# Fourier stage, last part: spectra of equal moving factor added on VectorE before the inverse transform along x

## The chip, the cores and the metric

The kernel runs on one core of one Trainium2 chip. The metric is the device time of one execution in microseconds. The engines have short names here, as in the profile: PE is TensorE's matmuls and PEld its weight loads, DVE is VectorE, ACT is ScalarE, POOL is GpSimd, SP is SyncE.

## The reference

The program is four layers of a metaformer on an input of 4 x 64 x 64 x 128 numbers in 32 bits. Every layer has a mixing part and a feed-forward part. The change lies in the mixing part of layer 2, a Fourier neural operator. Its last part works on 4 x 32 images of 128 x 128 points and applies, twice, one layer of this kind (`m0` and `m1`):

```python
def _spectral_conv(x, w2, oh, ow):
    w = w2[..., 0] + 1j * w2[..., 1]
    X = jnp.fft.rfft2(x, norm='forward')
    Xk = jnp.concatenate([X[:, :, :mh, :mw], X[:, :, -mh:, :mw]], axis=2)
    Yk = jnp.einsum('bixy,ioxy->boxy', Xk, w)
    ...
    return jnp.fft.irfft2(out, s=(oh, ow), norm='forward')

m = _fno_layer(an, m0cw, m0sw, H, W, inner_norm=True, act=True)
m = _fno_layer(m, m1cw, m1sw, H, W, inner_norm=True, act=False)
out = _inorm(m, mon_w, mon_b) + a
```

For each image, then: a transform to a few modes, a complex weight for each mode, a transform back, a normalization over the image, a scaled copy of the input added, and, in the first of the two layers, a Gelu.

## The kernel before

The stages of the four layers follow each other on one core. `stage_fourier` holds the Fourier operator, and its last part is a loop over 16 groups of images: four batches with four groups each, `group(b, g, pT)`, and eight tiles of 128 x 128 numbers in a group. All numbers are 32-bit floats.

A group is a Python generator. Its steps are cut by `yield`, and a loop at the end of the stage starts a new group every seven rounds and moves every active group on by one step each round. So the instructions of two or three groups alternate in the order in which they are recorded. A scheduler then settles the order on each engine; on an engine, instructions run in that order. Semaphores join the engines.

One group does this, with the lines of the profile:

- It loads its skip images (`sk`), adds the input image to them on POOL (L2089), and computes an inverse transform from `pT` (L2094, `ra`, `dya`) that is added (L2101). `pT` is rebuilt for each batch by 64 transposes (L2143, L2144).
- `image_stats` takes the moments (L2039 to L2053, with one matmul `pm`, L2044), `inv_std` and `shift` make scale and bias from them (L2058 to L2066), and `apply` writes eight tiles on ACT (L2071).
- `add_to_x` adds a result to the running x on POOL, in two instructions (L2079).
- For each of two layers it calls `spectral(m, mw[layer])`, then takes statistics of the result, applies the scale, adds the scaled input (L2125) and, in the first layer, applies the Gelu on ACT (L2127).

`spectral` is where the change is made. It handles a group in two halves of four tiles. For each half:

- four matmuls `prf` (L2006) transform along y; ACT copies the result to SBUF (`fr`, L2008);
- a matmul `pz` (L2014) transforms along x into a PSUM tile of 66 rows;
- DVE multiplies it by the weights in four instructions (L2018). The result is `m`, a tile named `w` in the profile, of 66 partitions with the axes u, c and 512 elements: `u` names which of two moving factors `rx[:, u, :]` the product meets in the inverse, and `c` the real or the imaginary part of the spectrum;
- `terms` makes the inverse along x: for each pair of images `j`, four matmuls (L2028) accumulate in one PSUM tile `pi`, over `u` and `c`;
- ACT copies `pi` (`ir`, L1991), and a matmul `pf` with `dyq` (L1997) ends the inverse along y.

The four products of one half are written so:

```python
nc.vector.tensor_tensor(
    m[:, u, c], window(pz, 32 * c, [[64, 8], [0, 2], [1, 32]]),
    window(f, 128 * u + 64 * c, [[0, 8], [32, 2], [1, 32]]), op=ALU.mult,
)
```

A matmul of 32-bit numbers leaves two records in the profile, so a call of `spectral` has 64 records at L2028, and the 32 calls have 2048.

Of the kernel before, what the change touches and what calls it, by code (L numbers as in the profile page):

```python
# [13 lines left out]
ALU = mybir.AluOpType  # L14
# [346 lines left out]
def window(ap, off, dims):  # L361

    return bass.AP(ap.tensor, ap.offset + off, [list(ap.ap[0])] + dims)
# [1191 lines left out]
def stage_fourier(k, a):  # L1555
# [11 lines left out]
    nc, tc = k.nc, k.tc  # L1567
    with ExitStack() as octx:
# [3 lines left out]
        def load(pool, name, shape, src=None, eng=None):  # L1572
            t = pool.tile(shape, F32, tag=name, name=name)
            (eng or nc.sync).dma_start(t, a[name] if src is None else src)
            return t
# [6 lines left out]
        rx = load(wp, "rx", [66, 2, 128])  # L1582
# [30 lines left out]
        with ExitStack() as ctx:  # L1613
# [8 lines left out]
            with ExitStack() as ctx2:  # L1622
# [76 lines left out]
                for b in range(4):  # L1699
# [50 lines left out]
                    for q in range(8):  # L1750
                        px = ps.tile([128, 4, 2, 33], F32, tag="pt", name="pxt")
                        for j in range(4):
                            for c in range(2):
                                for e in range(2):
                                    mark = nc.tensor.matmul(
                                        px[64 * e : 64 * e + 64, j].rearrange("p c m -> p (c m)"), rt[:, :, c, 32 * e + 4 * q + j], fw[:, c, :],
                                        start=(c == 0), stop=(c == 1),
# [29 lines left out]
            with ExitStack() as ctx2:  # L1787
                yp = ctx2.enter_context(tc.tile_pool(name="fo_y", bufs=3))
                ps = ctx2.enter_context(tc.tile_pool(name="fo_pss", bufs=2, space=PSUM))
                for hg in range(4):  # L1790
                    hs = slice(8 * hg, 8 * hg + 8)
                    acc = [ps.tile([128, 8, 64], F32, tag=f"acc{bp}", name=f"acc{bp}") for bp in range(2)]
                    for g in range(17):
                        n = 128 if g < 16 else 64
# [19 lines left out]
                    for bp in range(2):  # L1814
                        o = att[:, bp, hs, :]
                        m = yp.tile([128, 8, 1], F32, tag="m", name="m")
# [10 lines left out]
        with ExitStack() as ctx:  # L1827
# [58 lines left out]
            with ExitStack() as ctx2:  # L1886
# [25 lines left out]
                for q in range(16):  # L1912
                    acc = [ps.tile([128, 3, 132], F32, tag="acc", name=f"acc{bp}") for bp in range(2)]
                    for hp in range(16):
                        n = 2 * q + hp // 8
# [20 lines left out]
                    if q >= 8:  # L1936
                        u = sm.tile([128, 2, 4, 66], F32, tag="u", name="u")
# [15 lines left out]
        with ExitStack() as ctx:  # L1953
# [4 lines left out]
            for i in range(2):  # L1958
# [3 lines left out]
                for u in range(2):  # L1962
                    p, n = mc[:, 2 * u], mc[:, 2 * u + 1]
# [19 lines left out]
            def inverse(terms, dyi):  # L1983

                rs = []
                for h in range(2):
                    pi = ps.tile([128, 4, 128], F32, tag="pr", name="pi")
                    for j in range(4):
                        terms(pi[:, j, :], h, j)
                    r = sm.tile([128, 512], F32, tag="ir", name="ir", bufs=6)  # L1990
                    nc.scalar.copy(r, pi.rearrange("p j x -> p (j x)"))  # L1991
                    rs.append(r)
                yield
                pfs = []
                for r in rs:
                    pf = ps.tile([128, 4, 128], F32, tag="pf", name="pf", bufs=4)
                    nc.tensor.matmul(pf, dyi, r, start=True, stop=True)  # L1997
                    pfs.append(pf)
                return pfs

            def spectral(src, f):
                rs = []
                for h in range(2):
                    pr = ps.tile([128, 4, 128], F32, tag="pr", name="prf")
                    for j in range(4):
                        nc.tensor.matmul(pr[:, j, :], src[:, 4 * h + j, :], dyp, start=True, stop=True)  # L2006
                    r = sm.tile([128, 512], F32, tag="ir", name="fr", bufs=6)
                    nc.scalar.copy(r, pr.rearrange("p j c -> p (j c)"))  # L2008
                    rs.append(r)
                yield  # L2010
                ms = []
                for r in rs:
                    pz = ps.tile([66, 8, 2, 32], F32, tag="pr", name="pz")
                    nc.tensor.matmul(pz, fwp, r, start=True, stop=True)  # L2014
                    m = sm.tile([66, 2, 2, 8, 2, 32], F32, tag="w", name="w")
                    for u in range(2):
                        for c in range(2):
                            nc.vector.tensor_tensor(  # L2018
                                m[:, u, c], window(pz, 32 * c, [[64, 8], [0, 2], [1, 32]]),
                                window(f, 128 * u + 64 * c, [[0, 8], [32, 2], [1, 32]]), op=ALU.mult,  # L2020
                            )
                    ms.append(m)
                yield

                def terms(out, h, j):
                    for u in range(2):
                        for c in range(2):
                            nc.tensor.matmul(  # L2028
                                out, ms[h][:, u, c, 2 * j : 2 * j + 2].rearrange("p n a y -> p (n a y)"), rx[:, u, :],
                                start=(u == 0 and c == 0), stop=(u == 1 and c == 1),  # L2030
                            )

                return (yield from inverse(terms, dyq))

            def image_stats(src):
# [45 lines left out]
            def group(b, g, pT):  # L2081
# [36 lines left out]
                for layer in range(2):  # L2118
                    yield
                    pfs = yield from spectral(m, mw[layer])  # L2120
                    mean, var = yield from image_stats(halves(pfs))
                    r = inv_std(var)
                    y = tile8("m", 6)
                    apply(y, halves(pfs), r, shift(mean, r, 0.0))
                    nc.vector.scalar_tensor_tensor(y, m, par[f"m{layer}sw"], y, op0=ALU.mult, op1=ALU.add)  # L2125
                    if layer == 0:
                        nc.scalar.activation(y, y, AF.Gelu)  # L2127
                    m = y
# [20 lines left out]
            while True:  # L2149
                if rounds % 7 == 0 and waiting is not None:  # L2150
                    n = next(waiting, None)
# [738 lines left out]
```

## Time and profile before

| what | value |
|---|---|
| median of three runs | 6653.65 us (6647.25 to 6657.48) |
| the profiled execution, its time | 6648.12 us |
| its span, first to last instruction | 6646.1 us |
| mean granted clock of TensorE | 0.891 |
| PE busy | 5567.9 us, 84% |
| DVE busy | 4479.9 us, 67% |
| ACT busy | 3008.3 us, 45% |
| POOL busy | 2042.6 us, 31% |
| last part of the Fourier stage | 3355 to 4170 us |

The profile is of one execution, so sums are made against its 6648.12 us. Busy time is the time in which an engine has an instruction under way. The groups in part 5 give the line, the engine, the operation and the tiles, then count, total and mean duration, then how long the engine sat idle before them and what ended that. In a timeline each row has start, duration, engine, line, operation, tiles and count, and in brackets the idle time before it and what ended it. "PEclk" is the share of TensorE's full clock that was granted.

### The profile page before, as it was taken

The page shows a single profiled execution, that of the slowest core. Times are in us where ns is not written, and L with a number is a line of the kernel's source. Part 1 is how long each engine was busy: PE and PEld are TensorE (multiplying, and loading weights), DVE is VectorE, ACT ScalarE, POOL GpSimd, SP SyncE. Part 2 cuts the span into 40 slices and gives each one's busy share as a digit, 9 for nine tenths or more (in the row PEclk, how much of TensorE's full clock was granted, in tenths as well). Part 3 has the DMA queues.
Part 4 walks back from the last instruction along what each step waited for, and adds up shares of the span by engine and source line. Part 5 has one row for each costly group of instructions (what it writes and reads, how often), then busy time and mean ns, then how long its engine had stood idle before and what let it go on. Part 6 is the DMA issues. An engine that isn't in the chain of part 4 may idle for free. (4 is left out here: it accounts for less than half of the span.)

```text
span 6646.1 us, 144915 instructions
## 1 busy us (share of the span) xinstructions
PE 5567.9 (84%) x58031; PEld 3066.5 (46%) x58031; DVE 4479.9 (67%) x9659; ACT 3008.3 (45%) x6819; POOL 2042.6 (31%) x1806
## 2 busy tenths in 40 slices
PE   7777888866688858989978876898998998998989
PEld 3336666654456545334456655335235243252233
DVE  6748777754477562859945555884774866847877
ACT  5445555533155312731056565765234343352375
POOL 0002222210010100018921110353553654645645
PEclk9888889887799979989977788997997997989999
DMA  6556888870400022059700000001111111111101
GB/s 160 149 141 209 244 240 243 244 234 29 168 1 1 2 70 57 1 152 185 157 20 11 13 10 1 6 1 46 46 42 50 39 46 46 37 43 50 32 23 32
DMA packets 713463, 545.23 MB, mean 82 GB/s; under 512 B 299360, under 2 KB 624488, under 8 KB 709448
## 3 DMA queue, kind: packets, MB, share of 16 engines
q1 hardware_dynamic: 651464, 482.23, 27.1%
q10 hardware_dynamic: 61312, 53.57, 2.7%
q8 instruction: 463, 7.59, 0.5%
q14 instruction: 224, 1.84, 0.1%
HBM read 366.25 MB, written 152.86 MB: 78 GB/s over the span
## 5 line engine op out<-in xcount | busy, mean ns | idle before, releaser
L2706 DVE TENSOR_TENSOR t<-S,q 128x1536 f32<-128x1536 f32 x512 | 893.8, 1755 | 172.5 <-PE S L2706 172.2
L2706 POOL TENSOR_TENSOR t<-t,q 128x512 f32<-128x512 f32 x512 | 651.6, 1273 | 488.8 <-ACT t L2706 488.8
L2706 ACT COPY t<-S 128x512 f32<-128x512 f32 x512 | 299.7, 585 | 826.3 <-PE S L2706 768.2
L2706 PE MATMUL S<-R,L 32*128 32x512 f32 x4096 | 611.4, 651 | 44.0 <-DMA R<-wd 38.9
L2706 PE MATMUL acc<-t,sum 128*32 128x512 f32 x4096 | 548.0, 608 | 0.6 <-DVE t L2706 0.5
L2422 PE MATMUL pe<-ew,yT 128*128 128x512 f32 x1024 | 487.0, 611 | 27.3 <-DVE xs L2428 24.8
L909 DVE COPY_PREDICATED band<-bit,band 128x384 f32<-128x384 int32 (+11 forms) x384 | 312.4, 923 | 174.7 <-ACT band L900 156.1
L890 PE MATMUL S<-kpad,qm 32*64 32x192 f32 (+3 forms) x8192 | 360.8, 400 | 62.0 <-ACT band L900 23.0
L2428 DVE SCALAR_TENSOR_TENSOR xs<-pe,gate,xs 128x128 f32<-128x128 f32 x1024 | 331.3, 344 | 92.5 <-PE pe L2422 77.6
L2706 PEld LDWEIGHTS S<-R,L 32*128 32x128 f32 x4096 | 178.6, 186 | 462.0 <-ACT t L2706 391.4
L1928 PE MATMUL acc<-w,attT 128*64 128x396 f32 x2048 | 349.0, 500 | 25.7 <-issue 15.0
L2431 ACT ACTIVATE sc<-pe,gate 128x128 f32<-128x128 f32 x1024 | 290.3, 377 | 158.1 <-PE pe L2422 135.3
L1924 DVE TENSOR_TENSOR w<-xp,e 128x1188 f32<-128x1188 f32 x256 | 336.2, 1388 | 33.9 <-ACT xp L1907 14.6
L890 PEld LDWEIGHTS S<-kpad,qm 32*64 32x64 f32 x8192 | 261.4, 150 | 121.1 <-issue 60.4
L1001 PE MATMUL pt<-ident,D 128*128 128x128 f32 x1536 | 259.5, 318 | 64.2 <-DMA D<-dd 51.8
L2422 PEld LDWEIGHTS pe<-ew,yT 128*128 128x128 f32 x1024 | 181.6, 193 | 265.5 <-issue 168.4
L1923 POOL TENSOR_TENSOR w<-xtl,e 128x396 f32<-128x396 f32 x256 | 260.5, 1035 | 119.4 <-DMA e<-ed 75.6
L2028 PE MATMUL pi<-rx,w 66*128 66x128 f32 x2048 | 276.0, 291 | 10.1 <-DVE w L2018 2.9
L2028 PEld LDWEIGHTS pi<-rx,w 66*128 66x128 f32 x2048 | 253.1, 201 | 52.2 <-DVE w L2018 51.3
L1003 ACT COPY dt<-pt 128x512 f32<-128x512 f32 x384 | 205.5, 595 | 145.4 <-PE pt L1001 144.8
L2706 PEld LDWEIGHTS acc<-t,sum 128*32 128x32 f32 x4096 | 81.4, 108 | 391.7 <-issue 366.3
L1928 PEld LDWEIGHTS acc<-w,attT 128*64 128x64 f32 x2048 | 159.7, 137 | 215.1 <-issue 146.5
(529 smaller groups left out, 11442.7 us busy)
## 6 DMA issues: line engine op xcount, KB each, us to landing
vb<-vd SPq DMA_DIRECT2D x272, 256.0 KB
e<-ed SPq DMA_DIRECT2D x64, 792.0 KB
D<-dd SPq DMA_DIRECT2D x128, 192.0 KB
D<-dd SPq DMA_DIRECT2D x128, 168.0 KB
D<-dd SPq DMA_DIRECT2D x128, 144.0 KB
w<-in_e_weight_dram ACTq DMA_DIRECT2D x16, 1024.0 KB
w<-in_e_weight_dram SPq DMA_DIRECT2D x16, 1024.0 KB
D<-dd SPq DMA_DIRECT2D x128, 120.0 KB
```

The lines of the kernel that those rows point to most:

```text
L890: ins = nc.tensor.matmul(acc[g][64 * h : 64 * h + 64].rearrange("p (a s) c -> p a s c", a=3), qm[rows, h, m, :], keys, start=(m == 0), sto ...
L909: nc.vector.copy_predicated(flat[:, :, 0:n], bit[:, 0, :, i : i + 1].to_broadcast([128, 48, n]), flat[:, :, s : s + n])
L1001: ins = nc.tensor.transpose(pt[:, g, :], D[:, g, ty : ty + 382 : 3], k.ident)
L1003: nc.scalar.copy(dt, pt)
L1923: nc.gpsimd.tensor_tensor(w[:, 3:4], planes[q][:, 3:4], wide(1, [[132, 3], [1, 132]]), op=ALU.mult)
L1924: nc.vector.tensor_tensor(w[:, 0:3].rearrange("p b c m -> p b (c m)"), xp[:, q % 2], wide(3, [[1, 396]]), op=ALU.mult)
L1928: nc.tensor.matmul(acc[b // 2][64 * (b % 2) : 64 * (b % 2) + 64].rearrange("p c m -> p (c m)"), attT[:, b // 2, hp, 64 * (b % 2) : 64 * (b ...
L2028: nc.tensor.matmul(out, ms[h][:, u, c, 2 * j : 2 * j + 2].rearrange("p n a y -> p (n a y)"), rx[:, u, :], start=(u == 0 and c == 0), stop= ...
L2422: nc.tensor.matmul(pe[h].rearrange("p e c -> p (e c)"), yT[:, 128 * t : 128 * t + 128], ew[:, 4 * h : 4 * h + 4, :].rearrange("p e c -> p ...
L2428: nc.vector.scalar_tensor_tensor(xt, pe[0][:, e, :], gate[:, t, e : e + 1], xt, op0=ALU.mult, op1=ALU.add)
L2431: nc.scalar.activation(sc[:, e, j, :], pe[1][:, e, :], AF.Copy, scale=gate[:, t, 4 + e : 5 + e])
L2706: last[engine] = f(*args, **kw)
```

## The change

After the four products of a half, one VectorE instruction adds the two products that share the same moving factor (`c` = 0 and 1) for both `u`: 66 partitions, 2 x 512 elements. The sum lies where the product of `c` = 0 lay. `terms` then accumulates over `u` alone: two matmuls for each pair of images in place of four. The rest of the code is the same. The add is L2022 in the changed kernel; the matmul of `terms` is L2028 in both, and no other line that is named here changes its number.

```diff
                                 m[:, u, c], window(pz, 32 * c, [[64, 8], [0, 2], [1, 32]]),
                                 window(f, 128 * u + 64 * c, [[0, 8], [32, 2], [1, 32]]), op=ALU.mult,
                             )
+                    nc.vector.tensor_tensor(m[:, :, 0], m[:, :, 0], m[:, :, 1], op=ALU.add)
                     ms.append(m)
                 yield
 
                 def terms(out, h, j):
                     for u in range(2):
-                        for c in range(2):
-                            nc.tensor.matmul(
-                                out, ms[h][:, u, c, 2 * j : 2 * j + 2].rearrange("p n a y -> p (n a y)"), rx[:, u, :],
-                                start=(u == 0 and c == 0), stop=(u == 1 and c == 1),
-                            )
+                        nc.tensor.matmul(
+                            out, ms[h][:, u, 0, 2 * j : 2 * j + 2].rearrange("p n a y -> p (n a y)"), rx[:, u, :],
+                            start=(u == 0), stop=(u == 1),
+                        )
```

On the built program's order: SP and POOL issue the same instructions in the same order, and no engine's order changes outside this part of the stage.

## The prediction

> **What bounds the kernel now.** I read the page first (parts 1, 2, 5), then the windows view by stage, the timeline of single periods of the stage that is changed, and the clock in steps of 3.41 us. The edited loop runs only from 3355 to 4170 us of the 6646.1 us span; the chain of waits shown for the whole program ends in a later stage, so the edited stage has to be read by itself. It is no bandwidth stage: in it PE is busy 618.1 of 815 us, DVE 433.1, ACT 474.6, and nothing is full.
>
> The page has the edited matmuls, and the groups by shape have the row nearest to the new add:
>
> ```profile
> L2028 PE MATMUL pi<-rx,w 66*128 66x128 f32 x2048 | 276.0, 291 | 10.1 <-DVE w L2018 2.9
> ...
> L2664 DVE TENSOR_TENSOR s<-s,rs 128x1024 f32<-128x1024 f32 x32 | 37.4, 1209 | 36.8 <-PE pz L2659 36.6 <-issue 0.2
> ```
>
> There are two records for each matmul of the code: 64 records a call of `spectral`, 32 calls. The stage repeats itself: one Gelu (L2127) per group of images, sixteen in all, and between two of them lie two calls, first that of layer 1 of the older group (A), then that of layer 0 of the younger (B). I call this a period. Of the first fourteen, Gelu to Gelu, nine take 45.3 to 46.4 us; two take 57; three hold the transposes that build the next pT and take 53.0, 53.1 and 61.8. The fifteenth takes 44.2, and 35 us follow the last Gelu. The windows of one short and one long period:
>
> ```profile
> core 0: us, PE busy (x) PEld busy (x) DVE busy (x) ACT busy (x) POOL busy (x), PEclk, DMA share, GB/s
> 3799.16:3844.46 45.30, 34.26 (x220) 25.85 (x220) 26.43 (x96) 28.63 (x66) 7.57 (x6) 0.88 0.04 12
> 3642.84:3699.94 57.10, 46.13 (x220) 34.55 (x220) 26.76 (x96) 28.82 (x67) 7.62 (x6) 0.65 0.03 10
> ```
>
> The reader is to see the same instructions on all engines, 11.8 us apart, and a granted clock of 0.88 against 0.65: what PE's clock does in this stage is worth more than its instruction count. The timeline of the short period (Gelu starts at 3798.08) gives the path:
>
> ```profile
> 3799.19 3.58 PE L2006 MATMUL prf<-dyp,m 128*128 128x128 f32 x16 [6.89 <-ACT m L2127]
> ...
> 3803.66 4.87 DVE L2018 TENSOR_TENSOR w<-pz,f 66x512 f32<-66x512 f32 x8 [1.95 <-PE pz L2014]
> ...
> 3804.48 8.46 PE L2028 MATMUL pi<-rx,w 66*128 66x128 f32 x64
> ...
> 3812.78 1.95 PE L2006 MATMUL prf<-dyp,m 128*128 128x128 f32 x16
> ...
> 3814.56 1.88 PE L1997 MATMUL pf<-ir,dyq 128*128 128x512 f32 x4
> ```
>
> PE starts on the first products 0.8 us after VectorE, streams through all 64 records, and goes straight on to prf, pf, pz and call B. The first prf of the period runs at half clock (3.58 us against 1.95 later). In the long period it is call B that runs so:
>
> ```profile
> 3664.20 12.38 PE L2028 MATMUL pi<-rx,w 66*128 66x128 f32 x60
> ...
> 3681.26 3.25 PE L2094 MATMUL pi<-ra,pT 66*64 66x128 f32 x26
> ```
>
> against 7.34 and 1.74 us in the short one. Spacing of pi records from the weight loads: 6.55/58 = 0.113 us at full clock, 11.49/58 = 0.198 at half. The granted clock changes only on a grid of 3.41 us; so in steps of it:
>
> ```profile
> core 0: us, PE busy (x), PEclk, DMA share, GB/s
> 3662.46:3665.88 3.42, 3.08 (x19) 1.00 0.03 7
> 3665.88:3669.29 3.41, 3.41 (x18) 0.50 0.00 0
> ...
> 3819.48:3822.89 3.41, 3.30 (x27) 1.00 0.00 0
> 3822.89:3826.30 3.41, 3.41 (x33) 1.00 0.02 5
> ```
>
> The step before the drop held 15 records of pi, two of pm and two of pz that end in it (0.44 us); the step of 27 records, nearly all pi, kept the clock. And once it is halved, pi at 18 records a step (PE full) did not bring it back in the steps to 3686; 128-row matmuls (prf, pf) filling a step do, as at each period's start. So some 16 pi records in a step are too few.
>
> **The change, part by part.** The order of the built program stays the same on SP and POOL and outside this stage; PE, DVE and ACT differ in it alone.
>
> *Removed*: 32 of 64 records a call, 3.6 us of PE at 0.113. *Added*: two adds a call on VectorE over 66x1024 elements, both operands in SBUF; by L2664 1.2 us each (0.69 by L2101's 512 elements, 1.28 by L2125's 1024 with a scalar; L2664 has the same operation and size), 64 of them, 77 us. VectorE has room for these in 815 us; what counts is where they stand. The scheduler puts the first after five products, the second after the other three. *Moved*: each half's pi waits for all of its products and its add, and PE, in order, holds prf (A) or pi from pT (B) behind it. In B, pm now goes ahead of pi (free: pi waits longer), and pf of the first half goes between the two halves of pi, so it waits for an ACT copy.
>
> *Call A*, from the Gelu's start: products start at 5.58, spacing 0.60; five end at 8.7, add to 9.9, three to 11.7, add to 12.95. pi of half 0: 9.95 to 11.75; of half 1: 13.0 to 14.8. Before, prf began at 14.70. So at full clock the call gains nothing: +0.1 us. But PE now idles from the end of pz (6.56) to 9.95 and again from 11.75 to 13.0; every step of 3.41 us that covers most of the first gap has at most about 1.7 us of pz or 16 pi records. By the step at 3662 the clock drops by 12.4 at the latest. Then half 1 takes 16 x 0.198 = 3.2: +1.5 in all. prf at half clock (3.58 for 1.95): +1.6. prf and pf together then fill a step and bring the clock back within pf: +0.9 (0 to 1.7).
>
> *POOL*: its two adds xs<-xs,sk start at 8.99 and 10.53, beside the new adds. Such a collision exists in the trace: v<-mv is 0.17 us free and
>
> ```profile
> 3837.67 1.26 POOL L2079 TENSOR_TENSOR xs<-xs,m 128x512 f32<-128x512 f32 x1 [21.55 <-ACT m L2071]
> ...
> 3838.12 0.83 DVE L2051 TENSOR_TENSOR v<-mv 128x8 f32<-128x8 f32 x1
> ```
>
> beside POOL's add, ending with it; the products, with one operand in PSUM, are 0.67 with and without. The wait costs 0 to 1.2 a period; I take 1.0, since POOL, pushed back by the first add, ends its second near 12.7, where the second new add wants 11.7. So call B's products start 1.5 + 1.6 + 0.9 + 1.0 = 5.0 later: 24.2 for 19.26.
>
> *Call B*, from its first product: two statistics stand among the products, five end at 3.3, add to 4.5, three to 6.3, one reduction, add to 7.75. The clock has dropped again (one to two steps nearly empty). pi half 0 to 7.7, copy 0.7, pf 1.8 to 10.2, pi half 1 3.2 to 13.4, pi from pT 1.11 + 3.25 to 17.8, pf and two pf of the other inverse 2.0 + 3.6 to 23.4, pm to 24.0; from the last pm to the next Gelu the long period took 9.9 (3688.94 to 3698.86). 24.2 + 24.0 + 9.9 = 58.1: +12.8 on 45.3.
>
> *Sum*: nine short periods x 12.8 = 115; the two of 57, now some 58.4, 3; with pT, 62.9 for 53.0 twice and 61.8 once, 21; the two last periods and the start, with fewer or other calls behind them, 14 (0 to 25). 153 us on a profiled time of 6648.1 gives 6801; that execution is 5.5 us under the median 6653.65, inside the three runs' own spread of 10, so I say 6800 and carry no more.
>
> *A rule against the trace.* The step at 3662, in which PE had work in most of it, halved the clock. The Trainium skill, TensorE: Matmul & The Clock Gate, Part 1, says that the slow state comes after at least one idle window of about 3.4 us. By that rule the 3.4 us gap in A would hardly fill one, the clock would mostly stay, and the time would be that of rival 1; I go by the trace's step.
>
> **Rivals.**
> 1. *The clock stays full.* Then A costs 0.1 + 1.0 (POOL), and in B the variance and with it layer 1's apply (ACT, L2071) come 2.0 later, as both adds stand ahead of it on VectorE: +3.1 x 15 = 46, and the three long periods fall to the short ones (-11, -11, -9): +15, about 6665. For it: the drop hit only three calls before. Against: those calls had more pi records in a step than any call will have now. 0.08.
> 2. *A drops, B recovers*, in half or more of the periods: +5 to +8 each, 75 to 100 in sum: 6725 to 6750. The clock's steps run free of the kernel, so this differs by period. 0.17.
> 3. *Faster: the adds are cheap and the clock holds.* At L2101's 0.69 us for 512 elements instead of 1.2, A ends 1.05 earlier (13.65), B's delay is 1.0, no collision stays, and the long periods go: -31, about 6620. It decides if the add is under 0.8 us. Against: the same operation at 1024 elements is 1.21. 0.05.
>
> **How the numbers follow.** Forecast 6800 with 0.70: range of its own 6760 to 6850 (pf 0 to 1.7, POOL 0 to 1.2, the ends 0 to 25, and the clock coming back a step later). Down through rival 2 to part of rival 1, 6690 to 6850 leaves out about 0.18 (rivals 1 and 3, and the far tail). A measurement of this kernel can tell about 0.2% (13 us) from no change. Rival 1's 6665 lies at the edge of it: 0.05 same, 0.03 slower; rival 3 makes faster 0.05; slower 0.90.
>
> **What would show it.** In the profile after: L2022 x64 near 1.2 us; L2028 at 1024 records; periods of 57 to 60 us all alike; granted clock of the stage near 0.65 instead of 0.81; prf of call B at 3.5 us instead of 1.95; stage end some 150 us later, other stages unchanged. Periods of 48 us at 0.88 would make rival 1 right; an add well under 1 us would make rival 3's price right; periods above 62 would mean that pf does not bring the clock back.

## The result and the profile after

The changed kernel takes 6811.84 us (median of 4 runs, 6805.35 to 6827.85) against 6654.97 us of the kernel before (6647.25 to 6657.48): ratio 1.024, 95% interval 1.0223 to 1.0257. That is 157 us slower; 6800 had been predicted. The profiled execution took 6805.35 us with a span of 6803.2 us and a granted clock of 0.862 (before 0.891).

The groups by shape show that the change does what it says: half the records of the matmuls `pi` (L2028), and the new add, 64 times.

```profile
L2028 PE MATMUL pi<-rx,w 66*128 66x128 f32 x1024 | 219.5, 404 | 111.0 <-DVE w L2022 111.0
L2022 DVE TENSOR_TENSOR w<-w 66x1024 f32<-66x1024 f32 x64 | 85.1, 1330 | 0.6
```

The first line is the whole story in small. The count is halved, but PE's busy time in this line falls only from 276.0 to 219.5 us, because one record takes 404 ns instead of 291, and the idle time before it rises from 10.1 to 111.0 us, all of it ended by the add (L2022).

The stage itself in the windows view, from its start to the time at which it was over before, and the rest:

```profile
core 0: us, PE busy (x) PEld busy (x) DVE busy (x) ACT busy (x) POOL busy (x), PEclk, DMA share, GB/s
3355.00:4170.00 815.00, 553.40 (x2336) 416.24 (x2336) 439.99 (x1374) 421.79 (x942) 114.04 (x83) 0.65 0.03 9
4170.00:4323.00 153.00, 89.72 (x335) 64.77 (x336) 84.21 (x339) 60.08 (x138) 13.40 (x10) 0.61 0.02 6
```

The stage ends 153 us later, at a clock of 0.65 instead of 0.81. Gelu to Gelu, the first fourteen periods now take 57.4 to 59.3 us, and 62.8 with the transposes of the next pT. One period, in the timeline (the Gelu starts at 3867.11):

```profile
3868.22 3.52 PE L2006 MATMUL prf<-dyp,m 128*128 128x128 f32 x16 [6.77 <-ACT m L2127]
...
3875.63 1.21 DVE L2022 TENSOR_TENSOR w<-w 66x1024 f32<-66x1024 f32 x1
3876.09 3.11 POOL L2079 TENSOR_TENSOR xs<-xs,sk 128x512 f32<-128x512 f32 x2 [11.90 <-ACT sk L2071]
...
3876.99 2.70 PE L2028 MATMUL pi<-rx,w 66*128 66x128 f32 x16 [3.31 <-DVE w L2022]
3878.67 1.62 DVE L2022 TENSOR_TENSOR w<-w 66x1024 f32<-66x1024 f32 x1
...
3880.44 3.75 PE L2028 MATMUL pi<-rx,w 66*128 66x128 f32 x16 [0.75 <-DVE w L2022]
...
3883.98 3.62 PE L2006 MATMUL prf<-dyp,m 128*128 128x128 f32 x16
...
3887.39 2.38 PE L1997 MATMUL pf<-ir,dyq 128*128 128x512 f32 x4
...
3889.61 1.88 PE L2014 MATMUL pz<-fr,fwp 128*66 128x512 f32 x4
...
3890.67 0.69 DVE L2018 TENSOR_TENSOR w<-pz,f 66x512 f32<-66x512 f32 x1
...
3893.84 1.21 DVE L2022 TENSOR_TENSOR w<-w 66x1024 f32<-66x1024 f32 x1
...
3895.20 3.74 PE L2028 MATMUL pi<-rx,w 66*128 66x128 f32 x16 [2.59 <-DVE w L2022]
...
3901.49 3.62 PE L2028 MATMUL pi<-rx,w 66*128 66x128 f32 x16
...
3905.04 3.68 PE L2094 MATMUL pi<-ra,pT 66*64 66x128 f32 x32
...
3914.58 0.39 PE L2044 MATMUL pm<-st,blkh 128*128 128x48 f32 x2 [1.15 <-DVE v L2051]
```

PE waits 3.31 us for A's first add. Sixteen records then take 3.7 us, where at full clock 64 took 8.5; prf of call B takes 3.62 us instead of 1.95. The same stretch in steps of the clock (windows view again):

```profile
core 0: us, PE busy (x) PEld busy (x) DVE busy (x) ACT busy (x) POOL busy (x), PEclk, DMA share, GB/s
3871.31:3874.73 3.42, 2.35 (x8) 0.59 (x6) 2.10 (x4) 3.42 (x9) 0.00 (x0) 1.00 0.00 0
3874.73:3878.14 3.41, 1.15 (x10) 1.19 (x11) 3.41 (x6) 2.83 (x8) 2.04 (x2) 1.00 0.00 0
3878.14:3881.55 3.41, 2.66 (x13) 2.40 (x13) 2.12 (x2) 0.59 (x1) 1.07 (x1) 0.50 0.14 43
...
3888.38:3891.79 3.41, 3.11 (x8) 0.87 (x6) 2.84 (x11) 2.15 (x6) 0.00 (x0) 1.00 0.00 0
3891.79:3895.21 3.42, 0.43 (x3) 0.34 (x3) 3.42 (x7) 0.00 (x0) 0.00 (x0) 1.00 0.00 0
3895.21:3898.62 3.41, 3.41 (x16) 3.41 (x16) 3.31 (x8) 0.00 (x0) 0.00 (x0) 0.50 0.00 0
```

The first number behind the length is PE's busy time, and the 1.00 or 0.50 third from the end is the granted clock. The step in which A waits for its add has PE busy for 1.15 us, the one in which B waits 0.43 us, and both are followed by half clock.

### The profile page after: what moved, and what is told of

It reads as the page before. It is cut to its first block, busy times and chain, and to the rows that moved or that the text cites. A ratio compares the mean times of both kernels' runs of the same rounds, so it can differ in the third digit from the quotient of the medians.

```text
span 6803.2 us, 142971 instructions
## 1 busy us (share of the span) xinstructions
PE 5602.0 (82%) x57007; PEld 3092.1 (45%) x57007; DVE 4565.1 (67%) x9723; ACT 3010.8 (44%) x6819; POOL 2056.4 (30%) x1806
## 5 line engine op out<-in xcount | busy, mean ns | idle before, releaser
L890 PE MATMUL S<-kpad,qm 32*64 32x192 f32 (+3 forms) x8192 | 354.0, 394 | 68.6 <-ACT band L900 28.4
L2028 PE MATMUL pi<-rx,w 66*128 66x128 f32 x1024 | 219.5, 404 | 111.0 <-DVE w L2022 111.0
L2028 PEld LDWEIGHTS pi<-rx,w 66*128 66x128 f32 x1024 | 208.4, 308 | 146.9 <-issue 139.3
```

The source lines that it names most:

```text
L890: ins = nc.tensor.matmul(acc[g][64 * h : 64 * h + 64].rearrange("p (a s) c -> p a s c", a=3), qm[rows, h, m, :], keys, start=(m == 0), sto ...
L2028: nc.tensor.matmul(out, ms[h][:, u, 0, 2 * j : 2 * j + 2].rearrange("p n a y -> p (n a y)"), rx[:, u, :], start=(u == 0), stop=(u == 1),)
```

## The experiments

Theory C: the wait for the add thins PE's rows, the clock halves, and nearly all of the loss is that. Theory V: the loss is the add's own time on VectorE's path. Times are medians; "four periods" is Gelu to Gelu over four periods once the stage has settled, where it does.

**Fill the waits of after with matmuls that are overwritten.** A chain of matmuls of 128 rows, 12 ahead of the first half's matmuls `pi` and 4 ahead of the second's, in both calls.

```diff
+                    if j == 0:
+                        last = fill(out, last, (12, 4)[h], rs[1][:, 0:128])
                     for u in range(2):
-                        nc.tensor.matmul(
+                        with tc.issue_after(last.ins):
+                            last = nc.tensor.matmul(
```

> The changed kernel, with matmuls whose result is overwritten (128 rows, 128 columns) put into the gaps in which PE waits for the adds: 12 after pz, 4 between the two halves. Theory C (the halved clock of PE is most of the loss): the granted clock of the stage returns from 0.64 to 0.8 or more, periods to 46 to 49 us, time 6640 to 6690 us. Theory V (the adds make VectorE's part of the path longer, and the clock only goes along): the adds stay, so the time stays at 6790 us or more, with the clock up.

6691.33 us (6679.45 to 6710.05), ratio to before 1.0058 (1.0043 to 1.0074). More work on PE, with the same adds and the same waits for them, takes 120 us off the kernel after. The time is 1 us over C's range and 100 under V's. The clock of the stage rises to 0.80:

```profile
core 0: us, PE busy (x) PEld busy (x) DVE busy (x) ACT busy (x) POOL busy (x), PEclk, DMA share, GB/s
3355.00:4200.00 845.00, 598.39 (x3758) 468.74 (x3758) 516.04 (x1633) 484.54 (x1087) 132.82 (x96) 0.80 0.04 12
```

Some calls A still lose it, and their periods are the longer ones (49.8 to 53.2 us, for 46.5 to 48.3 elsewhere, the last and those with pT aside).

**Let before wait for an add, with all four matmuls of a pair kept.** Its result counts one spectrum twice.

```diff
+                    nc.vector.tensor_tensor(m[:, :, 0], m[:, :, 0], m[:, :, 1], op=ALU.add)
                     ms.append(m)
```

> The kernel before with the adds awaited, but all four matmuls of a pair kept (the output then counts one spectrum twice). The wait is the same as in the changed kernel, PE's work that of before. C: the gap of 3.4 us turns the clock down as well, and 64 records at half clock cost twice those of the change: periods near 66 us, 6920 to 6980 us. V: two calls a period, each 2.5 us longer and no more: 6720 to 6760 us.

6972.33 us (6970.21 to 6983.25), ratio 1.0481. Slower than after, by 160 us, as C asks: the wait brings the half clock, and twice the records then pass at it. V gave 6720 to 6760 and falls here.

```profile
core 0: us, PE busy (x) PEld busy (x) DVE busy (x) ACT busy (x) POOL busy (x), PEclk, DMA share, GB/s
3894.57:4167.64 273.07, 204.29 (x944) 168.85 (x944) 128.69 (x401) 122.63 (x273) 33.10 (x24) 0.64 0.03 8
```

**Put the adds aside in before.** The sum goes to a tile that nobody reads, so VectorE has the work and nobody waits.

```diff
+                    both = sm.tile([66, 2, 8, 2, 32], F32, tag="both", name="both", bufs=1)
+                    nc.vector.tensor_tensor(both, m[:, :, 0], m[:, :, 1], op=ALU.add)
                     ms.append(m)
```

> The kernel before, with the adds written to a tile that nobody reads: VectorE does the same work as after the change, PE waits for none of it and keeps its four matmuls. C: the clock stays near that of before (0.81 in the stage); only the statistics behind the adds come later, 0 to 2.5 us a period: 6655 to 6700 us. V: the adds themselves cost, 6780 us or more.

6677.16 us (6665.49 to 6685.67), ratio 1.0039 (1.0023 to 1.0055): within C's range; some 26 us for the adds' time alone, a sixth of the loss. Four periods take 197.99 us at a clock of 0.84, 6.9 us over before.

**Take the add out of after.** Half the matmuls `pi`, no add; one of the two summed products is left out of the result.

```diff
-                    nc.vector.tensor_tensor(m[:, :, 0], m[:, :, 0], m[:, :, 1], op=ALU.add)
                     ms.append(m)
```

> The changed kernel without the adds (the products of the imaginary part are left out of the result): two matmuls, no wait for an add. It shows what the removed matmuls are worth by themselves. C: each call ends some 3.5 us earlier as long as the clock stays: 6530 to 6600 us; if the thinner work of PE turns the clock down even so, 6600 to 6680. V: 6530 to 6560 us, whatever the clock does.

6650.31 us (6631.54 to 6658.94), ratio 0.9996 (0.9978 to 1.0013). Half of the stage's largest group on PE is gone and the median gains nothing. This is C's second branch; V's 6530 to 6560 is missed by some 90 us. The profiled execution, at 6634.21 us one of the faster ones, takes 699.5 us from first to last Gelu, for 739.5 and 717.7 in the two profiles of before, so the stage itself may gain a little. Four periods:

```profile
core 0: us, PE busy (x) PEld busy (x) DVE busy (x) ACT busy (x) POOL busy (x), PEclk, DMA share, GB/s
3593.60:3784.81 191.21, 130.53 (x688) 91.66 (x688) 109.33 (x385) 122.08 (x272) 30.39 (x24) 0.75 0.04 12
```

In before, four take 191.08 us with 944 records at 0.86. The 256 records fewer are paid back by the clock. In the period from 3784.8 call B loses it (its second half takes 3.19 us for 14 records) and the period takes 47.1 us; in the next one it doesn't (1.73 us), and it takes 42.9:

```profile
3808.65 3.19 PE L2027 MATMUL pi<-rx,w 66*128 66x128 f32 x14
...
3854.80 1.73 PE L2027 MATMUL pi<-rx,w 66*128 66x128 f32 x14
```

**Useful work in A's gap.** After, with the younger group advanced first in each round, so that B's prf stands between pz and `pi` of A.

```diff
-                for a_ in list(active):
+                for a_ in list(active)[::-1]:
```

> The kernel after with one thing else: in each round the younger group is advanced before the older one. TensorE's order becomes prf of A, pz of A, prf of B, products of A, pz of B, pf of A, products of B, so that B's sixteen 128-row products stand in the gap in which A's first products wait for the add. Nothing of the computation is changed. Theory C (the loss is the clock that halves because TensorE's rows thin out while the products wait): A's products now follow full work, so A keeps the clock, and B's first product comes at about 18.5 us after the Gelu instead of 23.6. If the clock also holds in B, the periods are 42 to 47 and the time 6590 to 6660; if it still halves in B's own gap (only two pf stand in it), the periods are 52 to 54 and the time 6720 to 6750. Rival N (it is the number of products that matters, whatever stands between them): the clock of the stage stays near 0.65, the periods near 57, the time 6790 to 6815.

6746.80 us (6740.50 to 6749.87), ratio 1.0151 (1.0128 to 1.0175): 65 us better than after, and inside the time of C's second branch. Its periods are less even than that branch has them, 49.1 to 56.8 us for 52 to 54, the last and those with pT aside. VectorE's first product of B comes 17.6 to 21.7 us after the Gelu (23.6 to 25.4 in after), in most periods later than the 18.5 expected, as many calls A still begin at half clock; the stage's clock is 0.69.

**The same order in before**, as a control, with the same diff.

> The control of the run before: the kernel before with the same other order of the two groups, nothing of the computation changed. If the order by itself is neutral: 6640 to 6660 with periods of 45 to 47. Theory C: prf of B behind pz of A leaves fewer thin stretches, so the three long periods (57, 61.8, 57.1) may go, which would be worth up to 35 us: 6610 to 6650. Rival: the order delays the older group's chain (pf, pm, Gelu of A come later): periods of 48 and more, 6680 and up.

6669.52 us (6663.11 to 6691.69), ratio 1.0046 (1.0031 to 1.0061). The long periods do go (44.1 to 51.2 us, no record of `pi` is at half clock), yet the short ones are 48.6 to 49.5, but for the first and the last. So the time lies in none of the three ranges, and the periods are on the rival's side, but not by its reason. In the settled periods B's first product comes 20.0 to 20.9 us after the Gelu, hardly later than in before (19.3 to 20.3); the loss lies behind it, 28.4 to 28.7 us to the next Gelu for 26.05. What delays call B there is not shown.

**Fill PE's idle time ahead of a period, in before.** 28, and in the second kernel 40, overwritten matmuls ahead of prf of call A.

```diff
                     pr = ps.tile([128, 4, 128], F32, tag="pr", name="prf")
+                    for _ in range(28 if h == 0 and f is mw[1] else 0):
+                        nc.tensor.matmul(pr[:, 0, :], dyp, dyp, start=True, stop=True)
```

> The kernel before with 28 matmuls of 128 x 128 added ahead of prf of A in each period; they write the place that prf then overwrites, so the result is that of before. They fill the idle time of about 10 us ahead of each period (3.75 + 6.64 us by the trace of before). Theory C: the clock is back, or is never lost, when prf begins: prf of A takes 1.95 instead of 3.68 us, so some 1.7 us x 15 = 25 us less, and some of the 31 us that the three long periods cost may go too: 6590 to 6630, clock of the stage over 0.9. If TensorE's clock at the beginning of a period is worth nothing, because another engine sets it: 6640 to 6655. If the added matmuls outlast the gap: 6655 to 6680.

> The kernel before with 40 instead of 28 overwritten 128 x 128 matmuls ahead of prf of A. In the run with 28, the periods before which they lasted until 1.5 us before prf had no half clock at all and took 44.7 us; the others lost the clock in the 5.4 us of idle time that the fast ones left. Theory C: with 12 more (2.8 us at full clock) no idle time over about 3 us is left, so all short periods take 44.5 to 45.5 and the three with pT transposes 51 to 53: 12 x 45 + 3 x 52 = 696 against 742 in before, 6590 to 6620. If the clock isn't what makes the difference between 44.7 and 47: 6650 to 6670 as with 28. If the matmuls outlast the gap: 6670 and more.

6665.81 us (6636.85 to 6701.99), ratio 1.0026 (1.0001 to 1.0051), and 6685.07 us (6672.69 to 6714.76), ratio 1.0064 (1.0040 to 1.0088). Both missed what I expected of C. Periods with hardly any half clock (a mean of 0.99 or 1.00) do take 44.7 to 46.7 us, but others take 57 to 62. With 40 the reason is visible: even where PE begins a period at full clock, it loses it inside the calls. Two steps after which the clock halved:

```profile
core 0: us, PE busy (x) PEld busy (x) DVE busy (x) ACT busy (x) POOL busy (x), PEclk, DMA share, GB/s
3559.41:3562.82 3.41, 3.08 (x23) 2.59 (x22) 3.41 (x7) 3.41 (x10) 0.10 (x1) 1.00 0.00 0
3822.23:3825.64 3.41, 1.27 (x3) 0.14 (x1) 3.41 (x12) 0.94 (x3) 2.44 (x2) 1.00 0.07 21
```

In the second, pz of call B waits 2.22 us for ACT's copy. In the first PE is busy nine tenths of the time, nearly all of it with 66-row matmuls. In this kernel a clock kept in one place is lost in another.

**Fill one call of after alone.** The fill of the first experiment in A only, and in B only.

```diff
-                        last = fill(out, last, (12, 4)[h], rs[1][:, 0:128])
+                        last = fill(out, last, (12, 4)[h] if f is mw[1] else 0, rs[1][:, 0:128])
```

> The kernel after with the overwritten 128-row matmuls of the first experiment in call A alone (12 ahead of the first products, 4 between the halves), none in B. If B loses the clock by its own gaps (theory C, as the prediction has it): A's products and B's prf run at full clock, B's products still at half: periods of 53 to 56, 6740 to 6785. If B only inherits the half clock from A's gap: about as with fills in both, 6680 to 6710. If A's gap costs nothing: 6800 and more.

> The kernel after with the overwritten 128-row matmuls in call B alone (12 ahead of the first products, 4 between the halves), none in A; the counterpart of the run with them in A alone (6746). Theory C: A goes as in after (half clock from A's gap on, B's prf at half), the fill brings the clock back in B: periods of 51 to 54, 6720 to 6755. If it is A's loss that makes the time: 6790 to 6815. If B's gap is all of it: 6680 to 6700, as with the matmuls in both.

A alone: 6746.01 us (6740.13 to 6749.07), ratio 1.0149 (1.0126 to 1.0173). B alone: 6743.39 us (6731.34 to 6755.51), ratio 1.0145 (1.0112 to 1.0178). Filling A saves 66 us, B 68, both 120 of the 157, so each call's own wait makes about half of what the clock costs. Periods take 51.3 to 59.1 us with A filled, where some calls A still lose the clock (53 to 56 expected), and 51.4 to 53.1 with B filled (51 to 54 expected), the last and those with pT aside. B does not merely inherit A's half clock, nor the other way round.

**Fill everything in after**: both calls and the 40 ahead of each period.

> The kernel after with the overwritten 128-row matmuls both in the calls (12 and 4, A and B) and ahead of prf of A (40): full clock through the whole stage, if theory C is right. What is then left of the change is the add's time on the way: by the run with the adds put aside about 2 us a period. Theory C: periods of 45 to 48, 6620 to 6670, and 20 to 40 above the run of before with the 40 matmuls. If the change has another cost that isn't the clock's: 6690 and more, as with the matmuls in the calls alone.

6682.95 us (6661.90 to 6705.25), ratio 1.0053 (1.0030 to 1.0075), the clock of the stage 0.90. It lies between the two ranges, 13 us over C's: this kernel too has periods that lose the clock (60.6 with pT, 53.6). And it is level with before under the same 40 matmuls (6685.07, on the same chip), where 20 to 40 more were expected. That does not make the change free. Its periods with little half clock take 47.3 to 48.6 us, as rival 1 of the prediction had it, against 44.8 to 46.7 in before with the 40: some 2 us a period remain for the adds. Before with the 40 loses the clock in four periods (57.3 to 61.9), which by these two profiles evens the totals out.

**Before again**, unchanged, for a second profile.

> The kernel before, unchanged, for a second profile of it. In the profile shown so far the stage from first to last Gelu takes 739.5 us with three long periods among the first six, and the first Gelu begins at 3385.5; in all the other profiles, whose code ahead of the stage is the same, it begins at 3393 to 3412. If the long periods belong to the kernel, the stage is again 735 to 745. If they come and go with the place of the clock's steps, some are missing: 707 to 730, with the first Gelu at 3395 to 3412. The run with the adds put aside (737.2, no long period) then has 10 to 30 us more in the stage than before has without them, which is what its ratio of 1.0039 asks for; if the stage is 740 again, that ratio comes from ahead of the stage and the adds cost nothing.

6642.29 us (6632.47 to 6660.55), ratio 0.9996 (0.9985 to 1.0007). The profiled execution has a span of 6658.4 us, its first Gelu at 3419.6 (34 us later than in the first profile, in the same code), one long period (57.2) instead of three, and 717.7 us from first to last Gelu instead of 739.5. So two of the long periods came and went, and the profile that the prediction started from owed its near-median total to a quick first part and a slow stage. It also clears up the adds put aside: their 737.2 us without a long period stand against 717.7 with one, so the adds do cost in the stage, some 20 to 30 us (19.5, and 11 to 12 more for the long period).

## Why the prediction was right

The side, the size and the mechanism came out, point by point in the period that starts at 3867.11 (times after the Gelu):

| step | predicted | measured |
|---|---|---|
| one add | 1.2 us, 0.69 to 1.28 | 1.21, 1.62 beside POOL |
| A's halves of `pi` start | 9.95 and 13.0 | 9.88 and 13.33 |
| clock halves in A | by 12.4 | 11.03 |
| prf of B, more than before | +1.6 | +1.6 (3.41 us to pf, for 1.78) |
| pf, more than before | +0.9 | +0.5 |
| VectorE's first product of B | 24.2 | 23.56 |
| B: first add ends, from its first product | 4.5 | 4.4 |
| B: second half of `pi` (L2028) ends | 13.4 | 14.4 |
| B: pi from pT ends | 17.8 | 18.0 |
| B: second pm ends | 24.0 | 24.3 |
| from there to the next Gelu | 9.9 | 9.6 |
| short period | 58.1 | 57.4 to 58.1 |
| period with pT | 62.9 | 62.8 |
| clock of the stage | 0.65 | 0.65 |

Three terms were mis-sized. The collision with POOL was put at 1.0 us; the second add of A took 1.62 instead of 1.21, so 0.4. It was mostly POOL that waited: its two additions to the image took 3.11 us together beside the new adds, for 1.26 us each elsewhere.

The nine short periods gave 104.9 us for 115. Of the 10 us, 5.7 are the base: the 12.8 were counted from 45.3, the shortest of the nine, whose mean is 45.9. The other 4.6 are the periods themselves, 57.6 on average for 58.1.

The third is the term for the ends of the stage. The two long periods gave 3.2 for 3, those with pT 20.5 for 21. What was left, the fifteenth period (+7.8), the first Gelu (+8.4) and all behind the last Gelu (+12.3), makes 28.5 for the predicted 14 and lies over its bound of 25. Of it 4.4 us arose ahead of the stage, in code that is the same; the repeat of before shows how little such a number from one profile means. The two misses, 10 too many and 14.5 too few, cancel: 157.1 for 153. The period was understood; that the sum came within 4 us is in part luck.

The base of the sum was weaker than the prediction said. It took the three long periods as a property of before; one profile more has one. Counted from there, the change costs 158 us between first and last Gelu instead of 136.

The rivals. Rival 1 (the clock stays, 6665) is what the fully filled kernel came nearest to (6683), and its period of 48 us was met; without the fill it doesn't happen. Rival 2 (B recovers, 6725 to 6750) has its image in the kernel with B filled, 6743, periods of 51.4 to 53.1; unfilled, no period of after recovers. Rival 3 (faster) has nothing for it: the add took the 1.21 us that the prediction went by, and even with no add at all the time is 6650.

The rule that was weighed (the Trainium skill, TensorE: Matmul & The Clock Gate, Part 1: the slow state after at least one idle window of about 3.4 us) would have led to rival 1. The steps above show PE busy for 1.15 and 0.43 us of the window, and in the kernel with 40 matmuls for 3.08 us, and the clock halved after each. Here the measurement decides, and going by the trace's own step was right.

## What to carry to other kernels

Fewer matmuls were no gain here, even without the add, as the thinner work of PE was paid for in clock: look at the granted clock of the stage, in its own steps, before counting instructions, and ask what a new wait leaves PE with for 3.4 us. In this stage an elementwise step put between two matmul groups cost its own time (some 26 of the 157 us) and the half clock for all that followed, until full 128-row work filled a step again. Overwritten full-row matmuls in the gaps took most of that back, useful ones in one gap 65 us; neither made the change a gain. Take the base of such a sum from two profiles, as where the clock falls differs from one execution to the next.

## What the runs showed of the hardware

*How much work keeps the clock.* For each step of 3.41 us between 3400 and 4130 us I added up the time that the matmul records took (0.43 us for 512 columns at full clock, by the spacing of the pz and pf records, in proportion for fewer; twice that at half clock, where the spacing is 0.85), each times its rows over 128 (the matmuls from pT, of which two start within 0.01 us of each other, at half of that), as a share of the step. In the fourteen profiles, 332 steps at full clock were followed by half clock, and 1415 by full clock. All of the 332 had a share of 0.44 or less, all but four 0.39 or less; of the 1415 all but one had 0.37 or more. So time weighted by rows separates the two, and busy time does not: a step nine tenths busy with 66-row matmuls lies below the line, and without the weight, steps with a share of up to some 0.75 were followed by half clock. Coming back needs twice as much: of 331 steps at half clock after which it returned, all but one had 0.75 or more; of the 930 after which it stayed, none had over 0.77. A stream of 66-row matmuls, however dense, has at most 66/128 = 0.52, so by these bounds it holds the clock and can't bring it back.

*The stage locks onto the clock's steps.* Where the periods settle, four of them (one batch, one with pT among them) take a whole number of steps of 3.413 us (22 steps took 75.09 us):

| kernel | four periods, us | steps | clock |
|---|---|---|---|
| before, both profiles | 191.08, 191.06 | 56.0 | 0.86 |
| before, 28 matmuls ahead of a period | 191.13 | 56.0 | 0.93 |
| after without the add | 191.21 | 56.0 | 0.75 |
| before, adds aside | 197.99 | 58.0 | 0.84 |
| before, younger group first | 198.09 | 58.0 | 0.84 |
| after, B filled | 215.04 | 63.0 | 0.75 |
| after | 235.48 | 69.0 | 0.64 |
| before, add awaited | 273.07 | 80.0 | 0.64 |

This would explain why taking out 256 records of 944, or adding 28 matmuls a period, left four periods the same within 0.2 us, and why the adds put aside, 16 x 1.2 us in four periods, came out as two steps. That a period which would end earlier waits for the same edge of the clock is argued from these numbers, not tried by itself. The kernels with A filled, with both calls filled, with 40 matmuls ahead of a period (before and after), and after with the younger group first did not settle so. None of the twelve kernels was faster than before.
